# A two-layer graph network with residual norms: what comes first in the prologue, and how the last stage adds its bias and normalizes

## The chip, the cores and the metric

The kernel runs on one core of a Trainium2 chip. The metric is the device time of one execution in microseconds (us); the median of three runs is used. A core has five engines, each with its own instruction stream in a fixed order: PE (matmul), DVE (VectorE), ACT (ScalarE), POOL (GpSimd) and SP, which issues most DMAs. ACT issues some DMAs too, and POOL issues the indirect ones.

## The reference

12,500 nodes with 256 features, 200,000 edges sorted by destination.

```python
edge_index = jnp.stack([src, dst])
x = _layernorm(x + _L0_gnn_ref(x, src, dst, edge_weight, ...))   # attention layer
x = _layernorm(x + _L1_gnn_ref(x, edge_index, ...))              # message layer

# layer 0: row = src, col = dst
feat = relu(einsum(feat_in, W) + b)                # self and neighbour part, 4 heads x 32 each
edge_w = (att_s[:, row] + att_n[:, col]) * adj_vals
agg = segment_sum(edge_w[..., None] * feat_nei[:, col, :], row)
feat = normalized per head (scale, offset), concatenated
# layer 1
messages = relu(concat([x[row], x[col]]) @ W_msg + b_msg)
aggregated = segment_sum(messages, col)
h = relu(concat([x, aggregated]) @ W_upd + b_upd)
return (h - mean) * rsqrt(var + 1e-5) * gamma + beta
```

## The kernel before

Edges are cut into 112 groups of 14 tiles of 128 edges (the last group has 9, the very last tile 64 edges). As edges are sorted by destination, a group needs one window of 128 nodes, whose first node is `base`; nodes are also cut into 98 blocks of 128.

**Stage layer 0 (L218 to L822).** For each group, the edges are sorted into blocks of their source node by comparisons and small products (`sort_tasks`), each edge's message is made by a product of a one-hot matrix with the window's features (`feat_tasks`), and rows of four messages are scattered into a log in HBM by POOL (L747). Edge data come in chunks of eight groups: `meta_load` loads 112 rows of 128 sources, destinations and weights (L311); `meta_tasks` casts them (`cast`, L325), turns them into columns on PE (`column`, L331), copies these out of PSUM on ACT (`keep`, L339), takes the block number and the place in the block (`block`, `place`, L349 to L354), splits the weight in three bfloat16 parts (`high`, `rest`, `mid`, `low`), subtracts the window's base (`windows`, L377), and counts pairs of edges of the same block (the "twins": `turn`, `pairs`, `mask`, `count`, L389 to L406).

The order of the work is written out by hand. The table `AT` gives each named piece of a group a time; the piece of group `g` is put at `256 g + AT[name]`, and the pieces of all groups are then issued in the order of these times (L798 to L822). Nothing is rescheduled later, so every engine executes its pieces in just this order. The first comparison of a group is `hot` (L588, the half that reads ACT's copy `bx`, made by `widen`, L584) and `hot_b` (L592); then come `ranks` (L600, PE), `quarter` (L603, ACT), `rows` (L607, DVE), `begins` (L611 to L615, PE), `keep_v` and `keep_begins` (L622, L619, ACT), `shift` (L625, DVE). `relu` (L475) writes `R`, read first by `att_mult` (L479).

Ahead of this list stands a prologue in program order: constants (L256 to L275), the windows' bases (`brow` loaded at L284, `bf` and `basei` at L287 to L292), loads of chunk 0, of groups 0 and 1 and of weights (L771 to L775), zeros for rows of the log (L776), the bases on all partitions by a product (L780 to L785), the bias of layer 0 split in three bfloat16 rows (L786 to L794; a product with three rows of ones adds it in PSUM, L464), and all of `meta_tasks(0)` (L795), twins included.

**Stage log (L912 to L1116).** For each block the log's rows are loaded, weighted and summed by products with one-hot matrices (L966, PE); heads and rows are normalized, `x1` is stored in HBM, and `pd`, the source half of the message product, too.

**Stage layer 1 (L1130 to L1401).** A step is a pair of tiles, 782 in all. POOL gathers `pd` rows by source, one gather for each tile (L1286), four steps ahead; DVE makes a one-hot matrix (L1310), PE the destination half (L1323), DVE adds (L1345), ACT applies relu (L1347), PE sums into `agg` (L1364). A `Side` list holds pieces of other work with a step as their due time; `pump` issues one between parts of a step, `end` what is left of the step. When a group's last step is done, `finish(g)` adds its pieces: `total`, `transposes`, `keep`, four update products (L1165), bias on DVE (L1170), relu on ACT (L1173), the first normalization (statistics L1177, aggregate L1182, root L1185, reciprocal and `nm` L1188 and L1190, `apply("h")` on ACT L1197), times gamma, plus beta, plus `x1` (three times L1202 on DVE), the second normalization with `apply("o")` and the store of the window (L1205, SP). For the last two groups the distances are shortened (`rate`, L1208). Windows of neighbouring groups overlap, and a later window's rows are the valid ones, so stores keep their order.

Of the kernel before, what the change touches and what calls it, by code (L numbers as in the profile page):

```python
# [18 lines left out]
FT = mybir.dt.float32  # L19
FR = mybir.dt.float32r  # L20
BF = mybir.dt.bfloat16
# [81 lines left out]
def kernel(  # L103
# [114 lines left out]
    with ExitStack() as l0:  # L218
# [34 lines left out]
                       allow_small_or_imprecise_dtypes=True)  # L253
        nc.gpsimd.iota(roww, pattern=[[1, RW]], base=0, channel_multiplier=RW,
                       allow_small_or_imprecise_dtypes=True)
        nc.vector.tensor_single_scalar(lessb, dpj, 0.0, op=OP.is_lt)  # L256
        nc.vector.tensor_single_scalar(less, dpj, 0.0, op=OP.is_lt)
        nc.vector.tensor_single_scalar(less4, less, float(RW), op=OP.mult)
        nc.vector.tensor_copy(identb, ident)
        nc.vector.tensor_copy(identr, ident)  # L260
        nc.vector.tensor_single_scalar(identk, ident, BIG, op=OP.mult)
        nc.vector.tensor_single_scalar(step, dpj, -1.0, op=OP.is_equal)
        nc.vector.tensor_tensor(step, ident, step, op=OP.subtract)
        nc.vector.memset(onesb, 1.0)
        nc.vector.tensor_single_scalar(pcol1, pcol, 1.0, op=OP.add)
        nc.vector.tensor_copy(iotab, iotac[:, None, 0:NBX].to_broadcast([P, GT, NBX]))
        nc.vector.tensor_single_scalar(iotar, iotac[:, None, 0:NR].to_broadcast([P, GT, NR]), 0.5 - NR / 2, op=OP.add)
        nc.vector.tensor_single_scalar(iotaq, iotac[:, :, None].to_broadcast([P, P, GT]), float(NR), op=OP.mult)
        nc.vector.tensor_tensor(later, iotac[:, None, 0:GT, None].to_broadcast([P, GT, GT, GC]),
                                iotac[:, 0:GT, None, None].to_broadcast([P, GT, GT, GC]), op=OP.is_gt)  # L270
        nc.vector.memset(ones3, 1.0)

        nc.vector.tensor_scalar(quart, pcol, NB - 0.5, float(GR), op0=OP.is_gt, op1=OP.mult)
        nc.vector.tensor_single_scalar(quart, quart, 0.5 - 0.5 / RW, op=OP.add)
        nc.vector.tensor_single_scalar(capc, pcol, float(CAPR), op=OP.mult)  # L275


        brow = dcp.tile([1, NG], I32, name="brow")
# [1 line left out]
        topc = dcp.tile([1, NG], FT, name="topc")  # L280
        nc.gpsimd.iota(topc, pattern=[[P, NG]], base=0, channel_multiplier=0,
                       allow_small_or_imprecise_dtypes=True)
        if NG > 1:
            nc.sync.dma_start(  # L284
                brow[:, 0:NG - 1],
                dst[0:(NG - 1) * GE].rearrange("(o g e) -> o g e", o=1, e=GE)[:, :, 0])
        nc.vector.memset(bf, 0.0)  # L287
        if NG > 2:
            nc.vector.tensor_scalar(bf[:, 1:NG - 1], brow[:, 1:NG - 1], float(N - P), None, op0=OP.min)
            nc.vector.tensor_tensor(bf[:, 1:NG - 1], bf[:, 1:NG - 1], topc[:, 1:NG - 1], op=OP.min)  # L290
        nc.vector.memset(bf[:, NG - 1:NG], float(N - P))
        nc.vector.tensor_copy(basei, bf)  # L292


        TC = GC * GT
# [7 lines left out]
        def meta_load(c):  # L303
            t0, nt, full = meta_span(c)
            raw[c] = []
            for i, ap in enumerate((src, dst, ew)):
                r = meta.tile([P, P], ap.dtype, name=f"mr{i}", bufs=1)
                if full < nt:
                    nc.vector.memset(r[:nt], 0)
                if full:  # L310
                    nc.sync.dma_start(r[:full], ap[t0 * P:(t0 + full) * P].rearrange("(r q) -> r q", q=P))  # L311
                if full < nt:
                    nc.sync.dma_start(r[full:nt, :E % P],
                                      ap[(t0 + full) * P:E].rearrange("(o q) -> o q", o=1))
                raw[c].append(r)
# [101 lines left out]
        def load_group(g):  # L417
            if g < NG:
                b = base_reg(g) if g else 0
                xw[g] = xin.tile([P, D], FT, name="xw")  # L420
                nc.sync.dma_start(xw[g], x[bass.ds(b, P), :])
            if g < NB:
                xb[g] = xin.tile([P, D], FT, name="xb")
                n = min(P, N - g * P)
                if n < P:
                    nc.vector.memset(xb[g], 0.0)
                nc.sync.dma_start(xb[g][:n], x[g * P:g * P + n, :])
# [127 lines left out]

        scatters, zeros = [], []
        zero = dcp.tile([P, RW * MW], FT, name="zero")
        nc.vector.memset(zero, 0.0)

        def zero_rows(r, n):  # L560

# [206 lines left out]
            return tasks  # L768


        meta_load(0)  # L771
        load_group(0)
        load_l0_consts()
        load_group(1)
        load_norm_consts()  # L775
        for r in range((NB - 1) * CAPR, NB * CAPR, P):  # L776
            zero_rows(r, min(P, NB * CAPR - r))
        nz0 = len(zeros)
        bp = ps.tile([P, 512], FT, name="fs")
        nc.tensor.matmul(bp[:, :NG], ones[0:1, :], bf, start=True, stop=True)  # L780
        nc.vector.tensor_copy(baseB, bp[:, :NG])
        nc.vector.tensor_scalar(baseP, baseB, pcol, None, op0=OP.add)
        nc.vector.memset(dcol, 0.0)
        if NG > 1:
            nc.vector.tensor_tensor(dcol[:, 0:NG - 1], baseB[:, 1:NG], baseB[:, 0:NG - 1], op=OP.subtract)  # L785
        parts = [dcp.tile([3, D], BF, name=f"b{k}") for k in range(3)]  # L786
        left = dcp.tile([3, D], FT, name="bl")
        nc.vector.tensor_copy(parts[0], b0b[:3])
        nc.vector.tensor_tensor(left, b0b[:3], parts[0], op=OP.subtract)
        nc.vector.tensor_copy(parts[1], left)  # L790
        nc.vector.tensor_tensor(parts[2], left, parts[1], op=OP.subtract)
        nc.vector.tensor_scalar(bias3, parts[0], ident[:3, 0:1], None, op0=OP.mult)
        for k in (1, 2):
            nc.vector.scalar_tensor_tensor(bias3, parts[k], ident[:3, k:k + 1], bias3, op0=OP.mult, op1=OP.add)  # L794
        for f in meta_tasks(0).values():  # L795
            f()

        work = defaultdict(list)  # L798

        def put_in(at, name, f):  # L800
            if f is not None:
# [320 lines left out]
    last1 = ctx.enter_context(tc.tile_pool(name="last1", bufs=1))  # L1122
    wus = last1.tile([P, 4, D], FT, name="wus")
    bub = last1.tile([P, D], FT, name="bub")
    gab = last1.tile([P, D], FT, name="gab")
    beb = last1.tile([P, D], FT, name="beb")
    nc.scalar.dma_start(wus, wu.rearrange("(c p) n -> p c n", p=P))
# [2 lines left out]
    with ExitStack() as l1:  # L1130
# [5 lines left out]
        def finish(g):  # L1136
# [23 lines left out]
            def upd(i):  # L1160
                def f():
                    if i == 0:
                        st["up"] = ps.tile([P, D], FT, name="up", bufs=1)
                    a = Q[g]["xT"] if i < 2 else st["aT"]
                    nc.tensor.matmul(st["up"], a[:, c[i % 2]], wus[:, i, :], start=(i == 0), stop=(i == 3))  # L1165
                return f

            def bias():
                st["h"] = fin.tile([P, D], FT, name="h", bufs=3)
                nc.vector.tensor_tensor(st["h"], st["up"], bub, op=OP.add)  # L1170

            def relu():
                nc.scalar.activation(st["h"], st["h"], AF.Relu)  # L1173

            def stats():
                st["bst"] = fin.tile([P, 6], FT, name="bst", bufs=4)
# [9 lines left out]

            def recip():
                nc.vector.reciprocal(st["rs"], st["rs"])  # L1188
                st["nm"] = fin.tile([P, 1], FT, name="nm", bufs=4)
                nc.vector.scalar_tensor_tensor(st["nm"], st["mv"][:, 0:1], -1.0, st["rs"],  # L1190
                                               op0=OP.mult, op1=OP.mult)

            def apply(name):
                def f():
                    nm = st["nm"]
                    y = st["h"] if name == "h" else fin.tile([P, D], FT, name=name)
                    nc.scalar.activation(y, st["h"], AF.Identity, bias=nm, scale=st["rs"])  # L1197
                    st[name] = y
                return f

            def elem(b, op):
                return lambda: nc.vector.tensor_tensor(st["h"], st["h"], b, op=op)  # L1202

            def store():
                nc.sync.dma_start(out[bass.ds(breg[g], P), :], st["o"])  # L1205
# [1 line left out]
            def add(work, s):  # L1207
                rate = {NG - 2: 0.7, NG - 1: 0.5}.get(g, 1.0)  # L1208
                at = lambda k: s + int(k * rate)
                work.add(at(1), total, shift)  # L1210
                work.add(at(3), transposes)
                work.add(at(4), keep)
                for i in range(4):
                    work.add(at(4 + i), upd(i))
                for k, f in enumerate((bias, relu, stats, aggr, root, recip, apply("h"), elem(gab, OP.mult),
                                       elem(beb, OP.add), elem(xw[g], OP.add), stats, aggr, root, recip,
                                       apply("o"), store)):
                    work.add(at(8 + k), f)

            return add  # L1220

# [133 lines left out]
        def stage_c(s):  # L1355
# [10 lines left out]
            if j + n == ntile[g]:  # L1366
# [5 lines left out]
                if g + 4 < NG:  # L1372
                    work.add(s + 5, lambda g=g: load_group(g + 4))

        check(work, last // 3)
        GA = 4
        for s in range(min(GA, last)):
# [239 lines left out]
```

## Time and profile before

| | us |
|---|---|
| runs shown: median (lowest to highest) | 4087.51 (4082.6 to 4089.36) |
| the profiled execution | 4089.95 |
| its span, first to last instruction | 4088.2 |
| busy: PE / DVE / ACT / POOL | 3580.6 / 3197.3 / 2465.8 / 2549.4 |
| chain that ended last, by engine | PE 34%, DMA 24%, DVE 23%, ACT 8%, issue 5%, POOL 4% |

A line of the timeline has start, duration, engine, source line, operation and tiles (out, then inputs), and in brackets the engine's idle time just before with what ended it. A `q` behind an engine's name is its sequencer, which issues DMAs. In tables by stage, busy time is followed by the number of instructions.

### The profile page before, as it was taken

To read this page: it belongs to the slowest core of one execution; us is meant where nothing else is said; L and a number is where in the kernel's file an instruction comes from. 1 tells how busy PE (TensorE), PEld (TensorE's weight loads), DVE (VectorE), ACT (ScalarE), POOL (GpSimd) and SP (SyncE) were. 2 spreads that over 40 slices of the span, in tenths; PEclk is the share of its full clock that TensorE was granted. 3 is DMA by queue.
4 is the path that set the end of the run, shared out by engine and by line. 5 is a ranking of instruction groups with operands and counts; after the bars stand their busy time and mean duration, and the time that the engine had idled before them with its cause. 6 is when DMAs were issued, how large, how long until landed. Compare 5 with 4: busy or idle time off the path is not lost.

```text
span 4088.2 us, 86328 instructions
## 1 busy us (share of the span) xinstructions
PE 3580.6 (88%) x26432; PEld 3016.1 (74%) x26432; DVE 3197.3 (78%) x9815; ACT 2465.8 (60%) x8632; POOL 2549.4 (62%) x2461
## 2 busy tenths in 40 slices
PE   7999999999989999999978878787888787787776
PEld 6888888887878888888866666666666666666665
DVE  8999999999878888888856666667666666666666
ACT  7999999999922222222246555555565555555555
POOL 2555555554455555555557777777777777777775
PEclk9999999999999999999999999999999999999999
DMA  5777766665566666666656666666666666666664
GB/s 183 261 259 260 258 221 209 208 209 192 195 204 183 186 185 180 184 186 185 182 148 169 171 171 171 169 171 171 171 170 172 169 173 168 169 173 169 169 171 129
DMA packets 457248, 763.85 MB, mean 187 GB/s; under 512 B 75772, under 2 KB 300574, under 8 KB 456782
## 3 DMA queue, kind: packets, MB, share of 16 engines
q1 hardware_dynamic: 326622, 415.17, 35.7%
q0 software_dynamic: 110848, 327.87, 26.2%
q10 hardware_dynamic: 19312, 15.21, 1.2%
q8 instruction: 216, 3.54, 0.4%
q14 instruction: 250, 2.05, 0.2%
HBM read 553.43 MB, written 204.54 MB: 185 GB/s over the span
## 4 chain that ended last, share of the span: by engine, by line
PE 34%; DMA 24%; DVE 23%; ACT 8%; issue 5%; POOL 4%; DVEq 0%; ACTq 0%; POOLq 0%; SPq 0%
DMA gb<-pd,srcf 21%; PE sum L966 20%; PE agg L1364 6%; DVE gb L1345 4%; POOL gb L1286 4%; ACT gb L1347 3%; DVE mv L685 2%; PE qp L1323 2%; PE qm L1054 2%; ACT junk L667 2%; DVE qh L690 2%; DMA rr<-reld 1%; DVE oT L725 1%; DVE A L592 1%; DMA reld<-rT 1%
## 5 line engine op out<-in xcount | busy, mean ns | idle before, releaser
L1286 POOL DMA_INDIRECT gb<-pd,srcf x1563 | 1510.2, 966 | 511.5 <-issue 266.8
L1364 PE MATMUL agg<-gb,o 128*128 128x256 f32 x3126 | 860.6, 398 | 271.5 <-ACT gb L1347 268.4
L1345 DVE TENSOR_TENSOR gb<-qp,gb 128x512 f32<-128x512 f32 x781 | 538.5, 690 | 653.6 <-DMA gb<-pd,srcf 501.0
L1347 ACT ACTIVATE gb<-gb 128x512 f32<-128x512 f32 x781 | 491.1, 629 | 797.6 <-DVE gb L1345 795.7
L747 POOL DMA_INDIRECT log<-m,ix x448 | 563.6, 1258 | 582.4 <-ACT m L741 386.9
L1364 PEld LDWEIGHTS agg<-gb,o 128*128 128x128 f32 x3126 | 556.0, 191 | 493.2 <-ACT gb L1347 433.3
L966 PE MATMUL sum<-lg,o 128*128 128x256 f32 x3724 | 836.8, 378 | 11.5 <-DVE o L958 11.5
L966 PEld LDWEIGHTS sum<-lg,o 128*128 128x128 f32 x3724 | 696.3, 189 | 109.3 <-POOL lg L953 11.7
L958 DVE TENSOR_SCALAR o<-iotap,lg 128x128 f32<-128x128 f32 x1862 | 627.9, 402 | 123.8 <-PE sum L966 113.8
L953 POOL TENSOR_TENSOR lg<-lg 128x512 f32<-128x512 f32 x392 | 410.3, 1059 | 418.7 <-DMA lg<-log 238.2
L1323 PE MATMUL qp<-qh,oT 128*128 128x256 f32 x1563 | 544.0, 370 | 2.1 <-DVE oT L1310 2.1
L667 ACT ACTIVATE junk<-wp,nbig 128x99 bf16<-128x99 f32 x1568 | 543.5, 352 | 1.9 <-PE wp L640 1.8
L734 PE MATMUL mp<-F,oT 128*128 128x132 bf16 x5376 | 406.4, 221 | 17.5 <-DVE oT L725 13.7
L1323 PE MATMUL qp<-ql,oT 128*128 128x256 f32 x1563 | 406.7, 283 | 0.0
L734 PEld LDWEIGHTS <-oT 128*128 128x128 bf16 x5376 | 349.6, 99 | 47.9 <-DVE oT L725 16.4
L667 ACT ACTIVATION_READ_ACCUMULATOR junk<-wp,nbig 128x1 f32 x1568 | 328.7, 210 | 0.0
L741 ACT COPY m<-mp 128x396 f32<-128x396 f32 (+1 forms) x672 | 313.7, 467 | 14.3 <-PE mp L734 13.9
L1323 PEld LDWEIGHTS qp<-qh,oT 128*128 128x128 f32 x1563 | 299.4, 192 | 20.3 <-DVE oT L1310 2.5
L1323 PEld LDWEIGHTS qp<-ql,oT 128*128 128x128 f32 x1563 | 299.5, 192 | 17.9
L1310 DVE TENSOR_SCALAR oT<-dr,baseP 128x256 fp32r<-128x256 int32 x782 | 288.7, 369 | 10.6 <-DMA dr<-in_dst_dram 10.6
L1331 ACT ACTIVATE o<-iotac,rel 128x128 f32<-128x128 f32 x782 | 266.0, 387 | 1.9 <-issue 1.5
L973 ACT COPY S<-sum 128x256 f32<-128x256 f32 x98 | 36.5, 373 | 337.6 <-PE sum L966 337.6
(253 smaller groups left out, 6429.5 us busy)
## 6 DMA issues: line engine op xcount, KB each, us to landing
lg<-log SPq DMA_DIRECT2D x392, 268.0 KB
dr<-in_dst_dram SPq DMA_DIRECT2D x781, 128.0 KB
rr<-reld SPq DMA_DIRECT2D x112, 512.0 KB
log<-zero SPq DMA_DIRECT2D x101, 268.0 KB
gb<-pd,srcf POOLq DMA_INDIRECT x1563
lg<-log SPq DMA_DIRECT2D x98, 201.0 KB
xw<-in_x_dram SPq DMA_DIRECT2D x112, 128.0 KB
xw<-x1d SPq DMA_DIRECT2D x112, 128.0 KB
```

Source lines behind the costliest of these rows:

```text
L667: nc.scalar.activation(small("junk", NBX, BF, p=P), st["w", i][:, k * NBE:k * NBE + NBX], AF.Relu, bias=nbig, accum_out=st["sl"][:, t:t + 1])
L734: nc.tensor.matmul(mp[:, r * (HD + H):(r + 1) * (HD + H)], st["oT"][:, r0 + r], F3[g][:, k], start=(k == 0), stop=(k == 2))
L741: nc.scalar.copy(st["m"][:, r0:r0 + n, 0:HD + H], st.pop(("mp", i))[:, :n * (HD + H)].rearrange("p (r w) -> p r w", r=n))
L747: ins = nc.gpsimd.indirect_dma_start(out=log[:, :], out_offset=bass.IndirectOffsetOnAxis(ap=st["ix"][:, k:k + 1], axis=0), in_=st["m"][:, ...
L953: e.tensor_tensor(t[:, 1, :n, 0:HD].rearrange("p r (h k) -> p r h k", h=H), t[:, 0, :n, 0:HD].rearrange("p r (h k) -> p r h k", h=H), t[:, ...
L958: nc.vector.tensor_scalar(o[:, r], iotap, t[:, 0, r, MW - 2:MW - 1], t[:, 0, r, MW - 1:MW], op0=OP.is_equal, op1=OP.mult)
L966: nc.tensor.matmul(sums[b], o[:, r], t[:, :, r, 0:HD], start=(k == 0 and r == 0), stop=(k == NK - 1 and r == n - 1))
L1286: nc.gpsimd.indirect_dma_start(out=gb[s][:r, i], out_offset=None, in_=pd[:, :], in_offset=bass.IndirectOffsetOnAxis(ap=srci[:r, t:t + 1], ...
L1323: nc.tensor.matmul(qp[:r, i], oT[:, i * P:i * P + r], q, start=(k == 0), stop=(k == 1))
L1345: nc.vector.tensor_tensor(z, qp, z, op=OP.add)
L1347: nc.scalar.activation(z, z, AF.Relu)
L1364: nc.tensor.matmul(agg[g], o[:r, i], z[:r, i], start=(j == 0 and i == 0), stop=lastmm)
```

## The change

At the beginning, constants are cut in four functions, of which the first is issued ahead of chunk 0's casts, the second between the columns and the block numbers, and two later. The loads of chunk 0 are issued ahead of that of the bases. ACT executes a copy of one element first. The first comparison of group 0 no longer stands behind the bases, zeros, bias split, weight parts, windows and twins of chunk 0: these are put into the list of work behind named pieces of group 0.

At the end, the update's bias is split in three bfloat16 rows once (in step 4) and added in PSUM by a product with three rows of ones ahead of the four update products; relu reads PSUM. The first normalization no longer has `apply("h")`: `centred` is (h - mean) times gamma and `scaled` is that times the reciprocal root plus `xb`, where `xb` = x1 + beta is made earlier (`rest`). A group's finish has 12 places in place of 16.

```diff
@@ constants @@
-        nc.vector.tensor_single_scalar(lessb, dpj, 0.0, op=OP.is_lt)
...
-        nc.vector.tensor_single_scalar(capc, pcol, float(CAPR), op=OP.mult)
+        def consts_first():
+            nc.vector.tensor_copy(iotab, iotac[:, None, 0:NBX].to_broadcast([P, GT, NBX]))
+            nc.vector.memset(onesb, 1.0)
+            nc.vector.tensor_single_scalar(lessb, dpj, 0.0, op=OP.is_lt)
+            nc.vector.tensor_single_scalar(less, dpj, 0.0, op=OP.is_lt)
+            nc.vector.tensor_single_scalar(less4, less, float(RW), op=OP.mult)
+            nc.vector.tensor_copy(identr, ident)
+            nc.vector.tensor_single_scalar(identk, ident, BIG, op=OP.mult)
+            nc.vector.tensor_scalar(quart, pcol, NB - 0.5, float(GR), op0=OP.is_gt, op1=OP.mult)
+            nc.vector.tensor_single_scalar(quart, quart, 0.5 - 0.5 / RW, op=OP.add)
+        def consts_second():
...
+        def consts_places():
...
+        def consts_pairs():
...
+        def first_load():
...
+        def first_nodes():
...
@@ prologue @@
+        warm = dcp.tile([1, 1], FT, name="warm")
+        nc.scalar.copy(warm, ones[0:1, 0:1])
         meta_load(0)
+        first_load()
         load_group(0)
         load_l0_consts()
-        load_group(1)
-        load_norm_consts()
...
-        for f in meta_tasks(0).values():
-            f()
+        consts_first()
+        mt = meta_tasks(0)
+        for n in ("cast0", "cast1", "col0", "keep0", "col1", "keep1", "col2", "keep2"):
+            mt["m_" + n]()
+        consts_second()
+        for n in ("block", "place"):
+            mt["m_" + n]()
...
         work = defaultdict(list)
+        for name, fs in (("hot_b", (first_nodes, lambda: load_group(1), load_norm_consts, bias_parts, bases)),
+                         ("rows", (mt["m_high"], lead_zero, mt["m_rest"], mt["m_mid"], mt["m_win"])),
+                         ("shift", (mt["m_turn"], mt["m_pairs"], mt["m_low"], consts_pairs)),
+                         ("att_mult", (mt["m_mask"], mt["m_count"])),
+                         ("centre", (consts_places, base_places))):
+            work[AT[name] + 0.5] += fs
@@ finish @@
                     if i == 0:
                         st["up"] = ps.tile([P, D], FT, name="up", bufs=1)
+                        nc.tensor.matmul(st["up"], one3, bub3, start=True, stop=False)
                     a = Q[g]["xT"] if i < 2 else st["aT"]
-                    nc.tensor.matmul(st["up"], a[:, c[i % 2]], wus[:, i, :], start=(i == 0), stop=(i == 3))
+                    nc.tensor.matmul(st["up"], a[:, c[i % 2]], wus[:, i, :], start=False, stop=(i == 3))
...
-            def bias():
+            def rest():
+                st["xb"] = fin.tile([P, D], FT, name="xb")
+                nc.vector.tensor_tensor(st["xb"], xw[g], beb, op=OP.add)
+
+            def relu():
                 st["h"] = fin.tile([P, D], FT, name="h", bufs=3)
-                nc.vector.tensor_tensor(st["h"], st["up"], bub, op=OP.add)
-
-            def relu():
-                nc.scalar.activation(st["h"], st["h"], AF.Relu)
+                nc.scalar.activation(st["h"], st["up"], AF.Relu)
+
+            def centred():
+                nc.vector.scalar_tensor_tensor(st["h"], st["h"], st["mv"][:, 0:1], gab,
+                                               op0=OP.subtract, op1=OP.mult)
+
+            def scaled():
+                nc.vector.scalar_tensor_tensor(st["h"], st["h"], st["rs"], st["xb"], op0=OP.mult, op1=OP.add)
...
-                for k, f in enumerate((bias, relu, stats, aggr, root, recip, apply("h"), elem(gab, OP.mult),
-                                       elem(beb, OP.add), elem(xw[g], OP.add), stats, aggr, root, recip,
-                                       apply("o"), store)):
-                    work.add(at(8 + k), f)
+                work.add(at(6), rest)
+                for k, fs in enumerate(((relu,), (stats,), (aggr,), (root, centred), (recip,), (scaled,), (stats,), (aggr,),
+                                        (root,), (recip, shifted), (apply,), (store,))):
+                    work.add(at(8 + k), *fs)
...
+        work.add(4, bias_parts)
```

`consts_second` holds capc, step, identb, pcol1 and the three rows of ones; `consts_places` iotar and iotaq; `consts_pairs` later; `first_load` the load of `brow`; `first_nodes` the instructions of L287 to L292; `bases` the product and `baseB`; `base_places` `baseP` and `dcol`; `lead_zero` the zeros and their five stores; `bias_parts` the seven instructions of the split.

## The prediction

> **What bounds the kernel now.** I read first the table by stage, made from windows of the span (columns: stage in us, length, then busy time and instructions of PE, PEld, DVE, ACT, POOL, granted clock, DMA share, GB/s).
>
> ```profile
> 0.00:34.00 34.00, 12.95 (x90) 9.68 (x90) 22.63 (x76) 10.49 (x40) 1.60 (x10) 1.00 0.45 126
> 34.00:100.00 66.00, 61.78 (x773) 52.30 (x774) 64.08 (x216) 64.72 (x319) 22.21 (x19) 1.00 0.64 213
> 100.00:1060.00 960.00, 919.84 (x11962) 796.27 (x11959) 935.95 (x3202) 932.65 (x4587) 493.94 (x385) 0.99 0.68 229
> 1140.00:2060.00 920.00, 907.52 (x4318) 790.15 (x4319) 788.75 (x2343) 195.40 (x455) 479.78 (x446) 0.99 0.64 183
> 2078.00:4064.00 1986.00, 1587.15 (x8230) 1290.91 (x8230) 1306.83 (x3717) 1171.80 (x2829) 1509.70 (x1563) 0.99 0.63 171
> 4064.00:4088.00 24.00, 6.76 (x26) 4.24 (x26) 10.43 (x41) 8.22 (x22) 0.53 (x1) 0.73 0.09 30
> ```
>
> Five stages, four limits. From 34 to 1060 us (layer 0) DVE is at 97%, and the second view, DVE's waits in 34 to 1060, names little beside one DMA; a DVE that never waits is a queue, so a microsecond won ahead of it stays won. From 1140 to 2060 PE is full (log sums, L966). From 2078 to 4064 it is POOL, though its busy share is only 76%: each of 1563 gathers is 0.966 us busy and 0.30 us on its way to the next.
>
> ```profile
> DVE oT L725 <- DMA rr<-reld: 10.8, 12, 5.3
> ```
>
> ```profile
> L1286 POOL DMA_INDIRECT gb<-pd,srcf x1563 | 1510.2, 966 | 511.5 <-issue 266.8 <-PE agg L1364 46.3 <-PE qp L1323 41.4
> ```
>
> 1510.2 + 0.30 x 1563 = 1979 of the 1986 us: the gathers follow each other without a wait for a buffer, so DVE, ACT and PE have slack there. What is left are the two ends. At the beginning DVE's timeline to 34 us (start, duration, idle before) shows an idle DVE behind the first groups' chains:
>
> ```profile
> 13.56 0.22 DVE L349 CAST mi<-srcf 128x112 int32<-128x112 f32 x1 [0.69 <-ACT srcf L339]
> ...
> 21.11 0.52 DVE L588 TENSOR_TENSOR A<-iotab,bx 128x693 bf16<-128x693 bf16 x1
> ...
> 23.56 0.15 DVE L607 TENSOR_SCALAR rows<-rows 99x1 f32<-99x1 f32 x1 [1.15 <-ACT rows L603]
> ...
> 26.39 0.22 DVE L625 SCALAR_TENSOR_TENSOR dl<-pos,capc,begun 99x1 f32<-99x1 f32 x1 [1.64 <-ACT begun L619]
> ...
> 31.43 0.43 DVE L479 TENSOR_TENSOR tm<-R,atb 128x256 f32<-128x256 f32 x1 [3.83 <-ACT R L475]
> ```
>
> At the end, ACT's timeline and the waits of the SP queue after 4070 us:
>
> ```profile
> 4077.91 1.09 ACT L1197 ACTIVATE o<-h,nm,rs 128x256 f32<-128x256 f32 x2 [0.80 <-DVE nm L1190]
> 4078.91 0.28 ACT L1185 ACTIVATE rs<-mv,epsn 128x1 f32<-128x1 f32 x1
> 4080.35 0.60 ACT L1197 ACTIVATE o<-h,nm,rs 128x256 f32<-128x256 f32 x1 [1.16 <-DMA out_dram<-o]
> ```
>
> ```profile
> SPq L1205 <- DMA out_dram<-o: 4.4, 3, 1.8
> ```
>
> The last three stores wait for one another: groups 109, 110 and 111 are stored at 4078.53, 4080.36 and 4082.70, each after the landing of the one ahead. So not the last group's arithmetic ends the kernel but the moment at which group 109's `o` is ready, plus three stores.
>
> **The beginning, step by step.** DVE's order in the built program has the same 76 instructions ahead of group 2's first comparison (L588, 33.80 us) as before, so the gain is the difference in idle time ahead of it. Before: 0.69 + 1.01 + 0.57 + 1.15 + 0.51 + 1.64 + 3.83 = 9.40 us (behind the initial 0.85 that both have). After, walked with the durations above:
> - SP issues the three columns first. Chunk 1's loads, issued at 35.09 with less traffic, had their packets in after 1.8, 1.7 and 1.8 us; src issued at 0.76 is then there by 2.6, dst by 3.0, weights by 3.5. DVE's first constants (iotab 0.8, seven more 1.5, the start at 1.4) end near 3.6, so the casts don't wait.
> - ACT now loads its table first (1.28 us, from the row at 7.34), copies one element, and only then issues w0, b0 and the two att loads: 1.06 + 0.75 + 1.23 us by their rows. It is free at about 5.4, while PE's first transpose is ready at 4.3. This is the price of the move, 1.1 us. The three copies out of PSUM stand 0.79 apart (13.28, 14.07, 14.86), so `bx` begins at 7.2 and the first comparison at 8.1 instead of 21.11. DVE idles 1.1 + 1.35 us on the way; the second constants fill the rest.
> - Behind it come the bases (1.0 us) and the bias split (2.63, from 9.90 to 12.53), which end at 13.4 with baseB: group 0's `rows` at 13.4 instead of 23.56. PE's product for the bases stands ahead of the first ranks (L600) and waits for DVE's bases; ranks start at 11.0, their result is out at 12.9, still ahead of DVE.
> - Group 1's first comparison waits 0.65 for `bx`, which now stands behind two casts on ACT; `dl` 0.15. The second and fourth waits above are gone because twins, `later` (1.75), pairs (1.0) now lie there. R comes at about 21.0 (ACT and PE, 10 us earlier than 31.01), where DVE has just ended group 1's second comparison: 0.5 idle, then 0.2 for `rows`.
> - Then mask and count (2.55) and places and base places (1.9) are paid, work that before lay ahead of 21 us. Group 2's comparison starts at 28.3.
>
> Idle after: 1.1 + 1.35 + 0.65 + 0.15 + 0.5 + 0.2 = 3.95; gain 9.40 - 3.95 = **5.45 us**. From there DVE's order is the old one. SP's moved pieces (group 1's windows at about 11.5 instead of 9.41, zeros after 14 instead of 10.52) have no reader before 25 us. Bounds: if the weights' load lands as late as it did before (about 6.6), the second att issue and all behind it slip by 1.9 and 3.5 are left; if ACT's five issues cost nothing beside PE, 6.5.
>
> [...]
>
> **Layer 1, the gathers.** Per group DVE loses the bias add (0.414) and a small `nm`, and three adds or products (L1202, 0.419 each) become one add and two scalar-tensor-tensor; ACT loses one `h` (0.585); PE gains one product with three rows (0.22 to 0.39 by the rows of L464). None of this is on POOL's path, which keeps its 1.27 us a gather unless the gathers themselves change. They can: by starts and durations in this trace, a gather beside a DVE instruction with two SBUF operands (L1202, L899, L1327) took 994 ns on average, the others 949. L1202's 326 instructions cover 262 gathers at 999 ns against 960: 10.3 us in all. After the change there are again three such instructions a group, so I take zero. Layer 0's scalar-tensor-tensor of this size (L493, 0.414) takes DVE as long as the add, which is the nearest row. Bounds: if the two new ones don't disturb at all, 2/3 of 10.3 is won, 6.9; if they disturb like the worst of the three (L899, 1022 against 962, 60 ns instead of 39), 175 x 21 ns = 3.7 are lost. [...] The split of the update's bias (some 2.7 us on DVE in step 4) is covered by POOL, which is four steps ahead, 10 us.
>
> **The end.** POOL's last gather, PE's last sums and group 111's `up` (ready at 4072.5, now 0.1 later by the bias product) stay. Before, group 109's second normalization stood on DVE behind 111's add, product and first statistics, and `o` began at 4077.91. After: relu straight from PSUM 72.65 to 73.06; statistics 73.12; 109's reciprocal and `nm` 73.5, 73.7; aggregates to 74.0; ACT: 111's root 74.05, then 109's `o` 74.25 to 74.85. Its store leaves at 4074.85 instead of 4078.53: **3.7 us**. 110's `o` is ready at 76.1 and waits for 109's landing (76.6); 111's (centred and scaled in two instructions of 0.42, root, reciprocal, `nm`, `o`) at 78.0, before 110's store has landed (78.9). So the three stores stay in a row and give back nothing. Bounds: 2.9 if 111's `o` and one more wait come late by 1 us, 4.3 if 109 slips ahead of 111's statistics.
>
> **Sum.** 5.45 + 0 + 3.7 = 9.15 us. The profiled execution took 4089.95 (span 4088.2 and 1.75 around it), so 4080.8 for it; it lies 2.4 above the median of 4087.51, which gives **4078.4**. A measurement of this kernel tells about 0.2% (8.2 us) from no change: the forecast lies just past that line, at 4079.3.
>
> **Rivals.** (a) Smaller gain: ACT's issues and late columns leave 3.5 at the beginning, the end gives 2.9, or DVE's twelve waits for `rr` (10.8 us, up to 5.3 each, where they fall is chance) fall worse: 4081.1 from the two bounds (6.4 us won), up to 4085 with one such wait more. For it: ACT's queue now stands between the columns and everything. Against: chunk 1's landings. (b) The two fused instructions leave POOL alone: 9.15 + 6.9 = 16.0, 4071.5. For it: no row shows a large scalar-tensor-tensor beside a gather of layer 1; against: it has two SBUF operands too. (c) Slower: the fused instructions hold POOL up much longer. To end 0.2% above, their 175 covered gathers must each lose (9.15 + 8.2) / 175 = 99 ns more than now, 138 in all; the worst row shows 60. Price then 4096 and more; that point decides, and nothing in the trace reaches it.
>
> **Chances.** Forecast 0.50 (of which 0.40 beyond the line, its own range 4075 to 4081), (a) 0.26, within 0.2%, (b) 0.17, (c) 0.07. Faster 0.57, same 0.36, slower 0.07. The range runs from (b), with 1.5 for the spread of the runs shown, to the end of (a): 4070 to 4085.
>
> **What would show it.** Group 2's first comparison on DVE at 28.3 (27.2 to 30.3), the first at 8.1; `o` of group 109 at about 3.7 us earlier after the last gather, three stores still in a row; gathers at 966 ns mean. A mean of 962 or 968 would speak for (b) or its opposite, each ns being 1.6 us. It is wrong if DVE after 34 us waits more than the 11 us of before, or if the layer 0 stage is not shorter by what DVE's first stage gained.

## Result and profile after

The change takes 4076.82 us (median of 13 runs, 4069.01 to 4078.8) beside 4087.51 of the kernel before (13 runs, 4080.59 to 4092.74): ratio 0.9974, 95% interval 0.9965 to 0.9982, so 10.7 us or 0.26% faster, just past the line of 0.2% and 1.6 us below the 4078.4 of the forecast. The profiled execution took 4078.69 us; its span fell by 11.3 us, from 4088.2 to 4076.9.

The table by stage of the kernel after (columns as in the table of before: stage, length, busy time and instructions of PE, PEld, DVE, ACT, POOL, granted clock, DMA share, GB/s):

```profile
0.00:34.00 34.00, 21.15 (x149) 16.13 (x149) 28.28 (x93) 17.41 (x71) 2.19 (x10) 0.90 0.50 143
34.00:100.00 66.00, 63.62 (x758) 54.44 (x758) 62.33 (x212) 61.97 (x305) 25.87 (x20) 0.90 0.65 217
100.00:1060.00 960.00, 920.22 (x11972) 796.88 (x11969) 935.59 (x3196) 933.77 (x4587) 493.01 (x387) 0.99 0.67 229
1140.00:2060.00 920.00, 907.98 (x4299) 790.02 (x4296) 784.93 (x2336) 194.66 (x456) 479.47 (x444) 0.99 0.63 182
2075.00:4057.00 1982.00, 1615.50 (x8342) 1311.13 (x8342) 1269.85 (x3511) 1117.73 (x2721) 1505.74 (x1563) 0.99 0.63 171
```

DVE does 93 instructions in its first 34 us in place of 76. New is the clock column: 0.90 up to 100 us, where before showed 1.00. The time stamps of both profiles say where the 11.3 us were won:

| us | before | after | earlier by |
|---|---|---|---|
| first comparison of group 0 | 21.11 | 7.94 | 13.2 |
| of group 2 | 33.80 | 27.79 | 6.0 |
| of group 5 | 62.14 | 58.45 | 3.7 |
| of group 111 | 1109.97 | 1105.77 | 4.2 |
| first log sum | 1155.44 | 1152.65 | 2.8 |
| first gather | 2078.37 | 2075.42 | 3.0 |
| first gather to end of last | 1986.16 | 1981.94 | 4.2 shorter |
| end of last gather to end | 23.65 | 19.55 | 4.1 shorter |

So 3.0 + 4.2 + 4.1, where the forecast had 5.45 + 0 + 3.7: the total came out near because two misses offset each other, which is luck and no proof of the terms.

The beginning, on DVE's timeline after (start, duration, idle before):

```profile
5.69 0.22 DVE L362 CAST mi<-srcf 128x112 int32<-128x112 f32 x1 [0.57 <-ACT srcf L352]
...
7.94 0.52 DVE L600 TENSOR_TENSOR A<-iotab,bx 128x693 bf16<-128x693 bf16 x1 [1.15 <-ACT bx L596]
...
14.92 0.52 DVE L600 TENSOR_TENSOR A<-iotab,bx 128x693 bf16<-128x693 bf16 x1 [0.61 <-ACT bx L596]
...
21.09 0.43 DVE L492 TENSOR_TENSOR tm<-R,atb 128x256 f32<-128x256 f32 x1 [0.95 <-ACT R L488]
...
27.79 0.52 DVE L600 TENSOR_TENSOR A<-iotab,bx 128x693 bf16<-128x693 bf16 x1
```

These four waits and one of 0.31 for `begun` (L637) are those of the prediction: 3.59 us in all, where it had 3.95, a last 0.2 included. Behind them DVE waits for ACT, which it hardly did before (columns: us in total, times, longest; 28 to 1060 us):

```profile
DVE oT L737 <- DMA rr<-reld: 10.7, 10, 5.1
DVE sl L686 <- ACT junk L679: 1.8, 3, 0.8
DVE rows L619 <- ACT rows L615: 0.9, 2, 0.6
```

The gathers' row (busy time and mean ns; idle), and at the end ACT's timeline and the waits of the last stores:

```profile
L1326 POOL DMA_INDIRECT gb<-pd,srcf x1563 | 1506.1, 964 | 511.5 <-issue 271.7
```

```profile
4067.30 0.58 ACT L1242 ACTIVATE o<-h,nm,rs 128x256 f32<-128x256 f32 x1
...
4070.54 0.60 ACT L1242 ACTIVATE o<-h,nm,rs 128x256 f32<-128x256 f32 x1 [0.47 <-DVE nm L1237]
```

```profile
SPq L1245 <- DMA out_dram<-o: 4.0, 3, 1.4
```

Group 109's `o` now begins 9.94 us behind the end of the last gather (13.38 before); the three stores still wait for one another, 4.0 us in place of 4.4. From the issue of 109's store to the end it is 9.00 us in place of 9.64: the third store follows the second by 1.83 us, not 2.34.

One thing is needed for what follows: the runs above had a granted clock of 0.99 over the whole span. Ten of the twelve experiments fell on chips that granted 0.92, where the kernel before itself takes 4542 to 4596 us; two at 0.98 to 0.99. Ratios are always to the kernel before on the same chip. Each time stamp below comes from one profiled execution of its kernel.

### The profile page after: what moved, and what is told of

It reads as the page before. It is cut to its first block, busy times and chain, and to the rows that moved or that the text cites. A ratio compares the mean times of both kernels' runs of the same rounds, so it can differ in the third digit from the quotient of the medians.

```text
span 4076.9 us, 86218 instructions
## 1 busy us (share of the span) xinstructions
PE 3617.4 (89%) x26544; PEld 3043.9 (75%) x26544; DVE 3156.6 (77%) x9599; ACT 2410.8 (59%) x8521; POOL 2546.2 (62%) x2461
## 5 line engine op out<-in xcount | busy, mean ns | idle before, releaser
L746 PE MATMUL mp<-F,oT 128*128 128x132 bf16 x5376 | 408.6, 222 | 16.8 <-DVE oT L737 13.7
```

The costliest lines, as they stand in the source:

```text
L746: nc.tensor.matmul(mp[:, r * (HD + H):(r + 1) * (HD + H)], st["oT"][:, r0 + r], F3[g][:, k], start=(k == 0), stop=(k == 2))
```

## Experiments

### Where the start's gain goes

**Beginning alone** (finish as before) and **end alone** (prologue as before):

```diff
 begin_only: hunks of constants, loads, zeros, prologue and list of work; finish(g) left as before
 end_only:   hunks of finish(g) and of the update's bias; prologue left as before
```

> The new beginning with the old finish. Theory (the start's gain is partly lost on the way): group 2's first comparison at 27.8 us as in the profile after (33.80 before), group 5's at 58.5, the first log sum only 2.8 to 3.0 us earlier than before's 1155.44, gathers at before's mean of 966 ns and the tail as before; 3 us in all, so about 4084.5. Rival (the prediction's step: what is won ahead of DVE's queue stays won, and the 3 us missing in the profile after are chance): the first log sum 5.5 to 6 us earlier, about 4081.8.

> The old beginning with the new finish. Theory (gathers and tail make the larger part of the change): the first gather at 2078.4 as before, gathers at a mean of 963.6 ns (4 us won over 1563), group 109's o about 3.5 to 4 us closer to the end of the last gather (9.9 us in place of 13.4), so about 8 us less than before, 4079.5. Rival (the prediction's sum: nothing on the gathers): mean of 966 ns, only the tail's 3.7, 4083.8.

Measured: begin_only 4585.34 us, ratio 0.9993 (0.9981 to 1.0005); end_only 4591.45, 0.9999 (0.9986 to 1.0013), at 0.92. Neither time confirms its theory: at that clock layer 1 has another limit (below). Nor can the marks of layer 1 be set beside a profile at 0.99: `o` of group 109 began 18.05 us behind the last gather in begin_only, 17.07 in end_only and 18.55 in product_only (below). The stamps of the start do tell something. Group 2's and 5's first comparisons: begin_only 27.74 and 58.40, as in the profile after, so that part is no chance; end_only 35.10 and 68.11, where before, with the same instructions up to there, had 33.80 and 62.14. The same order of work took 33.0 us from group 2 to group 5 in place of 28.3.

What differs is PE. Its rows for one form of product (columns: busy, mean ns of one) are given for three stretches of before, 20 to 30, 31 to 46 and 48 to 58 us, for end_only from 36 to 52 us, and for after from 20 to 30, 31 to 46 and 48 to 58 us:

```profile
L638 PE MATMUL wp<-v,identr 128*128 128x500 f32 x2 | 1.6, 777 | 0.3 <-ACT begun L619 0.3
```

```profile
L638 PE MATMUL wp<-v,identr 128*128 128x500 f32 x4 | 2.0, 497 | 1.8 <-ACT begun L619 1.3 <-ACT junk L667 0.5
```

```profile
L638 PE MATMUL wp<-v,identr 128*128 128x500 f32 x2 | 0.9, 474 | 0.0
```

```profile
L638 PE MATMUL wp<-v,identr 128*128 128x500 f32 x4 | 3.1, 786 | 0.5 <-ACT begun L619 0.3
```

```profile
L650 PE MATMUL wp<-v,identr 128*128 128x500 f32 x2 | 1.0, 496 | 1.2 <-ACT begun L631 0.7 <-ACT junk L679 0.5
```

```profile
L650 PE MATMUL wp<-v,identr 128*128 128x500 f32 x2 | 1.6, 786 | 0.1
```

```profile
L650 PE MATMUL wp<-v,identr 128*128 128x500 f32 x3 | 1.4, 479 | 0.0
```

In before the product takes 777 ns up to 30 us and 474 to 497 from then on; in end_only, with the same instructions, still 786 up to 52 us. In after it is fast from 20 us, slow again from 31 to 46, fast from 48. The granted clock of after says so too (PE's busy time is the first number behind the length):

```profile
24.00:28.00 4.00, 2.94 (x19) 1.60 (x19) 3.96 (x13) 1.92 (x10) 0.00 (x0) 0.87 0.02 5
28.00:32.00 4.00, 3.02 (x24) 2.80 (x23) 3.86 (x12) 2.66 (x15) 0.00 (x0) 0.50 0.44 144
32.00:36.00 4.00, 4.00 (x37) 3.47 (x36) 3.92 (x14) 3.90 (x14) 0.00 (x0) 0.50 0.00 0
...
44.00:48.00 4.00, 4.00 (x44) 3.58 (x44) 3.84 (x14) 2.65 (x14) 0.00 (x0) 0.57 0.00 0
48.00:52.00 4.00, 4.00 (x51) 3.24 (x49) 3.18 (x13) 4.00 (x21) 0.07 (x1) 1.00 0.66 211
```

PE runs at half its clock from 27.0 to 47.4 us. In the profile before, the column shows 1.00 from the start only because its first clock record is at 30.1 us; the 777 ns are the truth there. The next three were planned without this.

**Three edits of after around group 2.** The first operation on ACT a square root; constants of the places in DVE's early waits; two more comparisons on DVE:

```diff
 sqrt_first
-        nc.scalar.copy(warm, ones[0:1, 0:1])
+        nc.scalar.activation(warm, ones[0:1, 0:1], AF.Sqrt)
 places_early
             mt["m_" + n]()
+        consts_places()
...
-                         ("centre", (consts_places, base_places))):
+                         ("att_mult", ())):
...
+        work[AT["att_mult"] - 0.5].append(base_places)
 dve_delay
+        def delay():
+            for k in range(2):
...
-                         ("centre", (consts_places, base_places))):
+                         ("centre", (consts_places, delay, base_places))):
```

> The change after, but ACT's first one-element operation is a square root in place of a copy, so that the first table load may serve all and the one at 33.38 us (1.28 us) is gone. Theory (what the start won is lost on ACT, whose load stands between group 1's and group 2's picks, and DVE waits for these picks at 38.48 for 0.80 us): group 5's first comparison 0.8 to 1.3 us earlier than 58.4, at 57.1 to 57.6. Rival (ACT has slack there, the loss comes from PE's and DVE's own order): 58.4.

> The change after, with the two iotas of the places (1.3 us on DVE) put into DVE's wait of 1.15 us ahead of group 0's first comparison and the base places (0.6 us) into the wait of 0.95 ahead of group 1's tm. Theory (a microsecond won ahead of group 2 is only kept as far as ACT and PE follow): group 2's first comparison 1.9 us earlier, at 25.9, but group 5's only 0 to 1 us earlier than 58.4. Rival (DVE is the queue, as the prediction had it): group 5's 1.9 earlier, at 56.5.

> The change after, with two comparisons of the size of later (1.87 us each, results unused) added on DVE ahead of group 2's first comparison. Theory (behind group 2 the waits of DVE for ACT, 2.8 us between 36 and 50 us, take up what is won or lost ahead of them): group 2's at 31.5, group 5's only 1 to 2 us later than 58.4, at 59.4 to 60.4. Rival (DVE is the queue, a microsecond stays a microsecond): 62.1.

| | group 2 | group 5 | between | PE at half clock in between |
|---|---|---|---|---|
| before | 33.80 | 62.14 | 28.34 | 0 |
| end_only (order of before) | 35.10 | 68.11 | 33.01 | about 18 |
| after | 27.79 | 58.45 | 30.66 | 19.6 |
| less_two (below; order of after) | 28.63 | 59.78 | 31.15 | about 21 |
| more_two (below; order of after) | 28.56 | 59.70 | 31.14 | about 21 |
| sqrt_first | 27.82 | 58.48 | 30.66 | 19.9 |
| dve_delay | 30.81 | 59.23 | 28.42 | 10.2 |
| places_early | 25.46 | 54.96 | 29.50 | 12.8 |
| pe_fill (below) | 27.20 | 56.10 | 28.90 | 10.2 |
| places_fill (below) | 25.91 | 56.70 | 30.79 | 13.7 |

(Half clock by the clock records. The first record of end_only is at 53.2 us; there it goes by the same product, 786 ns from 36 to 52 us and 472 from 54 to 62. less_two and more_two have their first at 49.8 and 49.7, and the product at 784 to 788 ns up to 40 us.) The three ran once each, at 4538.38, 4533.20 and 4542.30 us beside 4542.68 of the kernel before, so only their stamps are read. sqrt_first lost only the second table load, and groups 2 and 5 did not move: my theory that ACT's load costs the microseconds fell, the rival held, though the clock there fell 3.2 us earlier than in after, which may hide a part. places_early won more than either theory had (3.5 us at group 5). dve_delay, put 3.0 us late at group 2, was 0.8 late at group 5, nearer to my theory (1 to 2) than to the rival (3.7); as places_early kept its gain, whether for the theory's reason is open. Both have 7 to 9 us less of half clock than after.

**Products that nobody reads, where PE waits between 22 and 30 us**, in after (pe_fill) and in places_early (places_fill), made to test the clock; each is a bf16 product of 128x128 by 128x512 into a free PSUM tile:

```diff
+        for at, n in ((412, 3), (464, 2), (491, 2), (547, 3)):
+            work[at] += [keep_busy] * n
```

> The change after, with ten products of 128x512 that nobody reads put on PE where it waits between 22 and 30 us: 3 behind group 1's begins, 2 behind its first place product, 2 behind its transposes, 3 ahead of group 2's ranks (about 2 us in all). Theory (the start's gain is lost because PE's granted clock falls to 0.50 at 27.0 us, behind a stretch of 3.4 us in which PE was 61% busy, and stays there to 47.4 us): the clock stays at 1.00, the stretch from group 2's to group 5's first comparison takes 28.3 to 28.8 us as in the profile before, not 30.7, so group 5's begins at 56.0 to 56.6 in place of 58.4. Rival (the clock falls after some microseconds at full speed whatever PE does, or DVE's waits for ACT there have another cause): 58.2 to 59.0.

> The same ten products together with the places' constants in DVE's early waits (as in the run that put them there alone, where group 2's first comparison began at 25.46 and group 5's at 54.96, with the clock at 0.50 for 10.2 and 3.4 us). Theory: the clock holds, 28.3 to 28.8 us from group 2's to group 5's first comparison, so 53.8 to 54.3. Rival: 54.96 or later, since DVE's waits go only to another place. Time beside the kernel before on the same chip: about 8 us less at group 5 than before, if the chip grants 0.99; at 0.92 not to be told from no change.

pe_fill, stretches of 4 us as above:

```profile
24.00:28.00 4.00, 3.78 (x29) 2.30 (x28) 3.93 (x14) 1.44 (x6) 0.00 (x0) 1.00 0.04 10
28.00:32.00 4.00, 2.33 (x21) 1.39 (x20) 3.90 (x10) 3.76 (x19) 0.00 (x0) 0.85 0.45 144
32.00:36.00 4.00, 3.67 (x34) 3.25 (x33) 3.63 (x16) 3.38 (x15) 0.00 (x0) 0.50 0.00 0
...
40.00:44.00 4.00, 4.00 (x51) 3.86 (x50) 3.79 (x11) 3.18 (x18) 0.00 (x0) 0.87 0.48 156
```

With PE busy for 3.78 of the 4 us from 24 to 28 the clock did not fall at 27.0. It fell at 30.8, behind the next sparse stretch (58% of 27.4 to 30.8), and for 10.2 us in place of 20.5. Group 5's came at 56.10, within the 56.0 to 56.6 expected, though the clock was not held throughout; 0.6 of the gain was there at group 2, and the stretch between took 28.90, 0.1 over the expected. pe_fill ran once (4586.53 us beside 4596.24). In places_fill the fill moved the fall to 33.8 and left 13.7 us of it; group 5's at 56.70 is 1.7 behind places_early, so there the expectation missed: much the same amount of half clock, but later, where groups 3 and 4 lie. Time of places_fill: 4582.78 us, ratio 0.9971 (0.9957 to 0.9985) at a clock of 0.918. It ran on another chip than the change's own second run, so whether it beats the change is open.

What do these show? That a slow PE costs time here: the old order took 28.34 us with none of it and 33.01 with 18 us of it. That filling PE's wait moves the fall: twice it came later. But the loss doesn't go by the time at half clock alone (10.2 us of it go with 28.42 and 28.90, 13.7 with 30.79, 19.6 with 30.66), and one order can have it or not: the clock of after's order rose at 20.1 us and fell at 27.0 in its own profile, while in less_two the product took 784 to 788 ns up to 40 us and the first record, at full clock, begins at 49.8.

### Layer 1

**Four more instructions a group on DVE**, with two SBUF operands or one:

```diff
+                for k in (2, 4, 9, 14):
+                    work.add(at(k), more)
 more_two: nc.vector.tensor_tensor(du, gab, beb, op=OP.add)
 more_one: nc.vector.tensor_reduce(du[:, 0:8], gab.rearrange("p (h k) -> p h k", k=32), AX.X, OP.add)
```

> The change after, with four additions of two SBUF tiles (gamma and beta rows, 128x256 f32, about 0.42 us each) more in every group, whose result nobody reads. Theory (each such instruction that falls beside a gather makes it longer by some 45 to 80 ns): 448 more of them at about 0.8 gathers each, 16 to 29 us longer, mean gather 974 to 982 ns, 4093 to 4106. Rival (the two-operand instructions only mark moments at which something else is slow): mean of 963 to 965, 4077 to 4079, since DVE has slack in this stage.

> The change after, with four sums over 32 columns of the gamma row (128x256 f32, one SBUF operand, about 0.41 us each as the sums of layer 0) more in every group, in the places where the earlier run had four additions of two SBUF operands. Theory (it is the second SBUF operand that makes a gather beside it longer): gathers at a mean of 960 to 964 ns, as without them, in place of the 979 ns of the run with additions. Rival (any DVE instruction of that length does it): 975 to 980 ns.

Their gathers:

```profile
L1332 POOL DMA_INDIRECT gb<-pd,srcf x1563 | 1530.4, 979 | 876.5 <-issue 543.2
```

```profile
L1332 POOL DMA_INDIRECT gb<-pd,srcf x1563 | 1511.0, 967 | 511.5 <-issue 261.7
```

By starts and durations, a gather beside one of the 448 additions (414 ns each) took 1040 ns on average and the others 963; beside one of the 448 sums (408 ns) 955 and the others 970. So it is the kind of instruction that counts, not that DVE is busy. The sum differs from the addition in its operation too, but the profile before has additions of the same size with one operand in PSUM: `qf` (L891), beside which alone 90 gathers took 946 ns, and the bias add (L1170). Of the 116 gathers beside the bias add, 96 also met an instruction with two SBUF operands and took 996 ns; the other 20 took 946. So the 995 ns that the expectation of product_only (below) gives for the bias add belong to instructions next to it. The mean of more_two is 17.6 ns over that of the change on a chip of like clock (961.5): 27.5 us over 1563 gathers, 61 ns for each addition. Its time, 4587.72 us, ratio 1.0000 (0.9986 to 1.0013), does not show it, against the 16 to 29 us of my theory, since at 0.92 POOL does not set the pace (below). more_one, at 0.98: 4083.45, 0.9972 (0.9962 to 0.9981), like the change.

**The bias as a product, norm as before**, and **the finish with gamma and beta left out** (its output lacks them):

```diff
 product_only: relu reads PSUM as after, then
+                for k, fs in enumerate(((), (relu,), (stats,), (aggr,), (root,), (recip, shifted), (apply("h"),),
+                                        (elem(gab, OP.mult),), (elem(beb, OP.add),), (elem(xw[g], OP.add),), (stats,),
...
 less_two: centring without gamma, x1 without beta
...
+                nc.vector.tensor_scalar(st["h"], st["h"], st["mv"][:, 0:1], None, op0=OP.subtract)
...
+                nc.vector.scalar_tensor_tensor(st["h"], st["h"], st["rs"], xw[g], op0=OP.mult, op1=OP.add)
...
-                work.add(at(6), rest)
```

> The change after, but with the old normalization: relu reads the product's bias from PSUM, then apply of h on ACT and three DVE instructions with two SBUF operands (gamma, beta, x1), sixteen places as before. Theory (a gather is longer beside a DVE instruction with two SBUF operands, and there are as many of these as before): gathers at 966 ns, as before. Rival (the dropped bias add, beside which gathers took 995 ns, was what disturbed): 964 ns or less. The tail loses most of its gain in both: group 109's o again more than 12 us behind the last gather.

> The change after, leaving out gamma and beta: no addition of beta ahead of the norm, and the centring subtracts the mean only (one SBUF operand). One instruction with two large SBUF operands is left in place of three. Theory: gathers shorter by the excess beside the two, 86 x 55 + 92 x 94 ns in the profile after, 8.6 ns a gather, or 58 x 72 + 68 x 24 ns = 3.7 ns by its second execution at a clock of 0.92: a mean of 955 to 958 ns in place of 961.5. Rival (the number of such instructions in the finish doesn't matter, the small difference between before and after is chance): 960 to 962.

product_only: 4587.76 us, 1.0005 (0.9992 to 1.0017). Its gathers took 961.0 ns, begin_only's 962.5 and end_only's 960.2 on the same chip; six kernels with one and the same finish gave 959.2 to 964.2 at 0.92. Differences of 2 ns are within that spread, so this doesn't tell which part brings what, and neither theory is borne out. The end it does tell: 28.29 us from the last gather to the end with the old finish, 29.00 with the product alone, and 23.16 to 26.64 in the eight executions at 0.92 that have the new norm. The shorter norm makes the end shorter, the product alone did not.

less_two: 4079.64 us, 0.9962 (0.9948 to 0.9976), gathers 963.4 ns, not the 955 to 958 expected. On that chip the gathers that meet no such instruction took 950.2 (more_one, same chip: 951.0), in the profile after 947.0. Beside more_one's 966.7 it is 3.3 ns or 5.2 us shorter: 2.5 ns of it are what gathers beside such instructions took beyond the others (24.6 us in more_one, 20.7 here). The number of such instructions does count, as more_two shows at full size, but the step I used, excess beside each row of one profile, overrated it, and the base moves by 4 ns between executions.

**The change again:**

> The change as it is, beside the kernel before on the same chip. The four runs so far came with a granted clock of 0.92 and 4588 us for the kernel before, and none of the parts moved that time by more than 0.1%. Theory (where PE's clock is granted at 0.92, layer 1 is PE's and not POOL's, and the change is worth only its start): ratio 0.999 to 1.000 if this chip grants 0.92 again, 0.997 if it grants 0.99 as in the profiles of before and after. Rival (the parts bring something only together): 0.997 at 0.92 too.

4534.54 us beside 4542.68: 0.9991 (0.9974 to 1.0008), clock 0.925. The theory held. Its layer 1 from 2300 to 4000 us, and its gathers:

```profile
2300.00:4000.00 1700.00, 1282.63 (x6087) 1073.58 (x6087) 917.85 (x2575) 812.35 (x1987) 1091.59 (x1137) 0.88 0.54 145
```

```profile
L1326 POOL DMA_INDIRECT gb<-pd,srcf x1563 | 1502.9, 962 | 870.2 <-issue 532.8
```

The gathers are as short as ever, but POOL idles 870 us between them in place of 512; they follow each other every 1.496 us, at 0.99 every 1.268. PE's clock is at half for 416 of these 1700 us (38 in the profile after). What is won on POOL or in a finish is then lost in such waits. That the clock causes all of them was not tried.

## Why the prediction was right, and where it was not

- **Up to group 2: right.** ACT free at 5.4 (5.40 measured), `bx` at 7.2 (7.13), first comparison at 8.1 (7.94), group 0's `rows` at 13.4 (12.95), group 2's at 28.3 (27.79). The price of ACT's early issues was counted where the trace shows it: `srcf` began at 5.40, 3.17 us after ACT's last operation, behind the issue of the att loads (4.04, 1.32).
- **"A microsecond won ahead of it stays won": failed.** 6.0 us at group 2 were 3.7 at group 5 and 2.8 at the first log sum. DVE waited 14.2 us from 28 to 1060 in place of 12.0 from 34 on, which the prediction had named as the sign of error. A queue that never waits is only one while its feeders keep up; DVE waits for ACT there, ACT for PE (3.6 us from 28 to 62, none in before from 34 to 62), and PE ran at half clock for 20 us. I had read the clock column as 1.00 throughout, and looked at no duration on PE. Half a microsecond came back by group 111, and 1.4 went between its comparison and the first log sum; that distance scatters from 44.3 to 46.9 us in the four profiles at 0.98 to 0.99, and why is open.
- **How much of the start's gain is kept is not settled by one pair of profiles.** Group 5 came at 62.14 in before and at 68.11 in end_only, with the same instructions but a slow PE up to some 53 us (the chip is not what makes it: begin_only, on end_only's chip, has after's stamps); after's 58.45 is 3.7 us ahead of the one and 9.7 of the other. Nor are the 3.0 us at the first gather repeated: more_one and less_two, with the same beginning, reach group 111 at 1109.73 and 1109.52 and the first gather at 2078.66 and 2077.16, where before had 1109.97 and 2078.37. Their chip took 6 us more for the kernel before, and there is no profile of it there, so this doesn't show that nothing is kept either.
- **Gathers 0: too low.** They won 4.2 us, inside the bound of 6.9, a mean of 963.6 ns in place of 966.2. The reading behind it, two SBUF operands, was borne out (955 ns beside the sums with one operand in more_one, 1040 beside the additions with two in more_two), and so was the count of three a group. Yet fewer gathers meet such an instruction, 624 in place of 705, and what these take beyond the others fell from 28.5 to 25.9 us; the others are 0.9 ns shorter, 1.5 us in all. At 0.92 fewer meet one too (543 to 559 in seven executions of the new finish, 625 with the old one), but without a smaller excess (19.3 to 23.2 us, and 21.9). With a spread of 4 to 5 ns between executions of one finish, that this gain belongs to the change is not shown. The two new instructions took 0.48 us each, not the 0.414 of L493.
- **The end 3.7: right in its mechanism, 4.1 measured.** `o` of groups 109 and 111 were forecast to begin 9.7 us and to be ready 13.5 us behind the last gather; the first began at 9.94, the other was ready at 13.8. So 109's store left 3.46 us earlier, and 0.64 came from the stores behind it, at which the forecast had nothing. The stores stayed in a row. The three profiles at 0.98 to 0.99 with a new finish agree: 19.55, 19.75 and 20.47 us from the last gather to the end, 23.65 before.
- **Rivals:** (c) fell, gathers grew at neither clock; (b)'s size was not reached; (a)'s smaller start came true in this pair of profiles, with a mechanism that no rival had.

## What to carry to other kernels

Here work won ahead of a busy engine was kept only as far as its feeders followed (6.0 us at group 2, 3.7 at group 5), and one of them changed its speed (PE's product took 496 ns in after's stretch from 20 to 30 us, 786 from 31 to 46): look at durations of one form of instruction over time, since a clock column without records shows 1.00 (in before up to 30.1 us, beside 777 ns). When a prologue is put forward, look at PE's clock in more than one execution: here the stretch behind the prologue took 2.3 us more in after than in before, and 4.7 more in another execution of the old order. And a gain on one engine is worth what it is only where that engine sets the pace, which on another chip, at another granted clock, it may not: the change gave 0.9974 at 0.99 and 0.9991 at 0.925, where POOL idled 870 us between its gathers in place of 512.

## What the runs showed of the hardware

- **PE's clock** was slow at the start of after: the product at 15.7 us took 787 ns, where it takes 474 to 497 at full clock (1.00 in the records of before and after) and 786 at half (0.50 in those of after). How long it takes to come up varies: in after two stretches of 3.4 us with PE 90 and 100% busy went ahead of the rise at 20.1, in more_two PE was 92 to 100% busy from 16 to 52 us, the product still took 786 ns from 31 to 46, and the first record, at full clock, begins at 49.7. The clock fell behind stretches that were 61% (after) and 58% busy (pe_fill, 27.4 to 30.8), but also behind 92% (places_early, at 41.7 us), and it stayed up behind 58% (begin_only, 2.33 of the 4 us from 56 to 60) and 59% (product_only, 2.35 there). So no share of busy time that decides comes out of these runs. All but the last record of before and of after last whole multiples of 3.41 us (3.41, 6.83, 20.48). In after PE was 95 to 100% busy in the five stretches of 3.4 us from 30.4 us on, and the clock stayed at half up to 47.4.
- **A DVE addition with two SBUF operands** made an indirect gather beside it longer, 1040 ns against 963 (more_two), 61 ns of POOL for each addition.
- **Chips differ**: the kernel before took 4087.51 to 4093.66 us where the clock was 0.98 to 0.99, and 4542 to 4596 where it was 0.92.
- **A square root as ACT's first operation** (sqrt_first): the second table load, 1.28 us at 33.38 in after, was gone (ACT was busy 2.77 us from 32 to 36, in after 3.90), to no effect on groups 2 and 5 (27.82 and 58.48 beside 27.79 and 58.45).
- **ACT's queue issued a DMA at 1.05 us** in after, while its table load ran from 0.75 to 2.03.
